# Four mixed blocks on images: operands in DRAM stored once and repeated by the reading transfer

## The chip, the core and the metric

The kernel runs on one core of one Trainium2 chip. The core has five engines that work side by side, each on its own list of instructions in a fixed order: TensorE multiplies matrices, VectorE (DVE) and ScalarE (ACT) work element by element, GpSimd (POOL) does the same and issues transfers, and the sync engine (SP) only issues transfers. They wait for one another through semaphores. Transfers between DRAM and the on-chip memory run on 16 DMA engines, whoever issues them. The metric is the device time of one execution in microseconds. All data are float32.

## The reference

The input is 16 images of 56 x 56 tokens with 128 channels. Four blocks follow, each on a group norm of the image and each added to it: attention in 7 x 7 windows, a triangle multiplication, a Fourier attention over tokens, and a bilinear block with depthwise convolutions. The change touches the end of the third and all of the fourth, which is, cut to what matters:

```
xp = silu(x @ W1) @ W2                 # q: 8 heads x 16, k: 16, v: 16
q, k, v = each normed over its 16 channels
K_H1   = conv3x7(k, H1, depthwise) + P1        # per token 16 x 16
kernel = einsum('xnk,xkd->xnd', q, K_H1)       # 8 x 16
F      = conv3x7(v, H2)                        # per token 16 x 16
V_G    = conv3x7(v, G) + I                     # per token 16 x 16
F      = einsum('xvw,xvd->xwd', V_G, F)
out    = einsum('xnd,xvd->xvn', kernel, F)     # 16 x 8 = 128 channels
```

In the third block the heads' results are sums over products of the image's spectrum with tables of weights, one table for each of 32 heads, the same for all images.

## The kernel before, in words

Images go through all four blocks one by one, and two lanes (even and odd images) have their own buffers, so that instructions of two images are mixed on every engine. The order on each engine is fixed when the program is built: a planner walks through the code with estimated times and places each instruction where it sees it ready. So two images can be in different blocks at the same time. Channels lie on the 128 partitions, tokens along them.

**Tables (third block).** At the start the weights of 32 heads are combined and written to a DRAM tensor `table` (L780, L809), ordered head, chunk, part, position. In the product loop each image runs over 8 chunks `q` and 8 groups `two`; for each, two transfers on GpSimd's queue (L1168) fill 56 partitions each with one copy of two heads' rows, 5376 bytes to a partition, taken from two places in DRAM. VectorE multiplies them with the spectrum (L1173) and TensorE sums.

**Contractions (fourth block).** A chunk is 448 tokens (8 rows), 7 chunks an image. The three einsums of the block all have one form: an operand `y` of 128 rows (a row for each pair of indices) and an operand `z` from a convolution. The products need each row of `y` on 8 partitions. [...] `kept` (L1284) copies `y` out of PSUM and writes it to a DRAM buffer, 8 copies of each row (L1288, on the ACT queue; 1792 KB). `contract` (L1372) then reads it back in four pieces `rep` of 128 partitions x 896 elements (L1381, on the SP queue; 448 KB each, three buffers in turn), VectorE multiplies each with `z` (L1384), and TensorE sums with a 0/1 matrix through the helper at L365 and L368. The sum is the next contraction's `y`. Per chunk there are three such contractions: queries with the key convolution, that result with the value convolution `l3wf`, and that with `l3wg` in `last`.

**Keys and values.** `project(q)` computes queries (kept as above), norms, and the 32 rows of keys and values of a chunk, and writes these to a DRAM tensor `padded` of zero-bordered planes, one plane for each of 32 channels x 3 row shifts x 7 column shifts, 672 in all: three transfers (L1338, on the ACT queue), each writing 7 shifted copies, 434 KB. `spread(q)` (L1344) reads the taps of one chunk back, 84 partitions x 4 groups, for keys and for values (L1347, on the SP queue, 651 KB each) into `im[0]` and `im[1]`, and `conv` (L1352) multiplies them on TensorE (L1362 for `l3wf`, otherwise through L365 and L368) and copies `z` out on ACT (L1369).

**The loop** (end of the block, L1423 on) does in step q: the last contraction of chunk q-2; the projection of chunk q+2; convolution and contraction of `l3wf` and then convolution `l3wg` for chunk q-1; `spread(q)`; convolution `l3wk` and the first contraction for chunk q. At the program's start 672 planes for each of two lanes are filled with zeros (L1256 to L1262).

Of the kernel before, what the change touches and what calls it, by code (L numbers as in the profile page):

```python
# [42 lines left out]
P = 128  # L44
T = 56
# [259 lines left out]
def tile_blocks(ctx: ExitStack, tc: tile.TileContext, ins, out, at, stages=(0, 1, 2, 3)):  # L305
# [41 lines left out]
    def dram():  # L347
        return dyp[lane[0]].tile([P, 8 * CH], F32, tag="dy", name=uid("dy"))
# [365 lines left out]
def _fourier(env):  # L714
# [65 lines left out]
    table = e.dpool.tile([32, 8, 3, STEP], F32, tag="table", name="table")  # L780
# [28 lines left out]
    for c, v in enumerate((cvr, cvi, tmp)):  # L809
        nc.sync.dma_start(out=table[:, :, c, :], in_=v.rearrange("p (c n) -> p c n", n=STEP))  # L810
    sc = W("sc")
    tflat = table.rearrange("h c k n -> h c (k n)")
# [299 lines left out]
    def run(b, xt):  # L1112
# [46 lines left out]
        for q in range(8):  # L1159
# [4 lines left out]
            for two in range(8):  # L1164
                t = slots[n % 8]
                n += 1
                for hh in range(2):
                    nc.gpsimd.dma_start(  # L1168
                        out=t[hh * T : (hh + 1) * T, :].rearrange("p (u n) -> p u n", u=2),
                        in_=bc(tflat[4 * two + hh : 4 * two + hh + 3 : 2, q, :], 0, T),  # L1170
                    )
                t4 = t.rearrange("p (u k n) -> p u k n", u=2, k=3)
                tt(t4, bc(x3[:, :, s], 1, 2), t4, ALU.mult)  # L1173
                prods = [t[:, u * 672 : (u + 1) * 672] for u in range(2)]
                group = []
                for p, k, m in ((pa, 0, 2 * STEP), (pb, 2 * STEP, STEP)):
                    for half in (1, 0):
                        pair = 2 * two + half
                        group.append(
                            dict(  # L1180
                                out=p[64 * half : 64 * half + 64, :m],
                                lhsT=at[:, pair % 8, pair // 8, :],
                                rhs=prods[half][:, k : k + m],
                                start=two == 0,
                                stop=two == 7,
                            )
                        )
                e.together(group)
# [58 lines left out]
def _bilinear(env):  # L1247
# [8 lines left out]
    padded = [e.dpool.tile([P, 672 * PLANE // P], F32, tag=f"padded{k}", name=f"padded{k}") for k in range(2)]  # L1256
    zeros = e.arena()
    part = 672 * PLANE // P // 3
# [9 lines left out]
    def run(b, xt):  # L1268
# [15 lines left out]
        def kept(p):  # L1284
# [3 lines left out]
            nc.scalar.dma_start(out=d.rearrange("p (k t) -> p k t", k=8), in_=bc(t[:, :CH], 1, 8))  # L1288
            return d

        def project(q):
# [45 lines left out]
            for dr in range(3):  # L1337
                nc.scalar.dma_start(  # L1338
                    out=planes(kv_dram, (1 + 8 * q) * PITCH + dr * (7 * PLANE - PITCH), ((21 * PLANE, 32), (PLANE - 1, 7), (1, SPAN))),
                    in_=bc(t, 1, 7),  # L1340
# [3 lines left out]
        def spread(q):  # L1344

            for i in range(2):
                nc.sync.dma_start(  # L1347
                    out=im[i][:84].rearrange("p (g t) -> p g t", g=4),
                    in_=planes(kv_dram, 336 * i * PLANE + q * SPAN, ((PLANE, 84), (84 * PLANE, 4), (1, SPAN))),
# [22 lines left out]
        def contract(y, z):  # L1372

            acc = e.psb()
            yv = y.rearrange("(i n a) (k t) -> n (a k) i t", n=2, a=D, k=8)
            for n in range(2):
                done = []
                for two in (0, 2):
                    rep = reps[count[1] % 3].rearrange("p (i t) -> p i t", i=2)
                    count[1] += 1  # L1380
                    nc.sync.dma_start(out=rep, in_=yv[n][:, two : two + 2, :])  # L1381
# [41 lines left out]
        queries, kern, feat = {q: project(q) for q in range(2)}, {}, {}  # L1423
        for q in range(NCH + 2):
# [4 lines left out]
            if 0 <= q - 1 < NCH:  # L1429
                f = kept(contract(kern.pop(q - 1), conv("l3wf", 1)))  # L1430
                feat[q - 1] = f, conv("l3wg", 1)
            if q < NCH:
                spread(q)
                kern[q] = kept(contract(queries.pop(q), conv("l3wk", 0)))
# [26 lines left out]
```

## Time and profile before

| | |
|---|---|
| time, median of 3 | 15542.86 us (15519.85 to 15596.55) |
| span of the profiled execution | 15563.9 us |
| mean granted TensorE clock | 0.760 |
| DMA bytes | 2251.47 MB, mean 145 GB/s |
| kept operands L1288 | 336 transfers of 1792 KB |
| operand reads L1381 | 1344 of 448 KB |
| keys and values L1338 | 336 of 434 KB |
| taps L1347 | 224 of 651 KB |
| table reads L1168 | 2048 of 294 KB |
| products L1384 on VectorE | 1344 of 2018 ns, 2668.4 us |

A busy share is an average over stages with different limits, so it says little alone. The view of stretches gives the busy time of each engine, the clock and the share of time in which the 16 DMA engines have a packet, for any stretch of the span. The view of waits says for how long an engine stood idle ahead of the instructions of a line, and whose work ended last before it went on; a transfer is written `to<-from`, so `arena<-dy` is a read of a kept operand, `dy<-w` the write, `arena<-padded` a read of taps, and `padded<-arena` the write of keys and values. The chain goes back from the last instruction, at each step to what released it. Packet counts of a queue hold one packet for each contiguous piece and 16 signals for each transfer; q10 is the ACT queue, q1 the SP queue, q0 GpSimd's.

### The profile page before, as it was taken

What the parts mean: (1) busy time and instruction counts of PE and PEld (TensorE: products, weight loads), DVE (VectorE), ACT (ScalarE), POOL (GpSimd) and SP (SyncE); (2) the same over time, 40 slices, a digit from 0 to 9 for tenths busy, and PEclk for the clock granted to TensorE, in tenths of its full rate; (3) what the DMA queues carried; (4) which work ended last, traced back from release to release, by engine and by line L of the source; (5) the groups of instructions that cost most, each with busy time, mean ns of one, the idle gap of its engine ahead of it and who ended that gap; (6) DMA issues with size and microseconds to landing.
All of it is one profiled execution on the core that took longest, in us unless ns stands there. A gap on an engine that the chain in (4) does not pass through costs nothing. (4 is left out here: it accounts for less than half of the span.)

```text
span 15563.9 us, 217025 instructions
## 1 busy us (share of the span) xinstructions
PE 11864.3 (76%) x91360; PEld 6531.3 (42%) x91360; DVE 9494.0 (61%) x13537; ACT 3743.0 (24%) x6251; POOL 1616.6 (10%) x2554
## 2 busy tenths in 40 slices
PE   7887677876888777877778777787777877778675
PEld 4453254443444334534345334453443534435332
DVE  6655666656666656566565665756657566574654
ACT  3222131221321222212222122231221312213111
POOL 0120002200022000210001100111102011020110
PEclk8876787767777678777787777877777777787766
DMA  2356904468145661466533655427465274651747
GB/s 73 79 125 188 299 24 107 110 207 262 34 102 159 189 214 50 98 167 190 170 104 84 190 167 170 135 71 211 129 190 144 57 207 117 190 150 51 217 126 228
DMA packets 1148653, 2251.47 MB, mean 145 GB/s; under 512 B 90656, under 2 KB 1030944, under 8 KB 1145760
## 3 DMA queue, kind: packets, MB, share of 16 engines
q1 hardware_dynamic: 552336, 840.48, 18.4%
q0 software_dynamic: 165120, 629.67, 17.0%
q10 hardware_dynamic: 430224, 767.43, 15.2%
q8 instruction: 722, 11.83, 0.3%
q14 instruction: 251, 2.06, 0.0%
HBM read 1412.72 MB, written 811.60 MB: 143 GB/s over the span
## 5 line engine op out<-in xcount | busy, mean ns | idle before, releaser
L1384 DVE TENSOR_TENSOR arena<-arena 128x1792 f32<-128x1792 f32 x1344 | 2668.4, 2018 | 1468.3 <-DMA arena<-dy 788.1
L368 PE MATMUL psb<-arena,cst 128*32 128x448 f32 (+1 forms) x10368 | 1971.0, 681 | 10.6 <-DVE arena L1216 10.3
L1173 DVE TENSOR_TENSOR arena<-arena 112x1344 f32<-112x1344 f32 x1024 | 1571.1, 1553 | 514.5 <-DMA arena<-table 502.1
L1168 POOL DMA_DIRECT2D arena<-table x2048 | 1326.1, 649 | 3611.6 <-PE psb L1087 990.2
L365 PE MATMUL psb<-arena,cst 128*32 128x448 f32 (+1 forms) x1728 | 1089.8, 720 | 728.1 <-DVE arena L1384 567.9
L368 PE MATMUL psd<-arena 112*64 112x224 f32 (+1 forms) x6144 | 1504.6, 477 | 0.0
L365 PE MATMUL psd<-arena 112*64 112x448 f32 x2048 | 1140.7, 644 | 211.9 <-DVE arena L1173 203.0
L368 PEld LDWEIGHTS psd<-arena 112*64 112x64 f32 x6144 | 617.5, 156 | 605.0 <-issue 596.1
L365 PE MATMUL psd<-arena,wgt 85*32 85x448 f32 x896 | 491.1, 680 | 488.1 <-DMA arena<-padded 486.3
L368 PEld LDWEIGHTS psb<-arena,cst 128*32 128x32 f32 (+1 forms) x10368 | 571.9, 141 | 652.5 <-issue 584.7
L1369 ACT COPY arena<-psd 128x896 f32<-128x896 f32 x336 | 304.2, 905 | 1913.3 <-PE psd L368 930.0
L663 PE MATMUL psd<-wgt,arena 128*64 128x128 f32 x7168 | 616.4, 326 | 164.8 <-DVE arena L675 121.7
L365 PEld LDWEIGHTS psb<-arena,cst 128*32 128x32 f32 (+1 forms) x1728 | 206.6, 154 | 1148.2 <-DVE arena L1384 625.5
L663 PEld LDWEIGHTS psd<-wgt,arena 128*64 128x64 f32 x7168 | 521.0, 165 | 351.7 <-issue 251.1
L1064 DVE TENSOR_TENSOR arena<-w,coef 128x1792 f32<-128x1792 f32 x256 | 507.4, 2019 | 215.6 <-PE psb L368 198.8
L884 PE MATMUL psb<-cst,arena 128*64 128x32 f32 (+1 forms) x10752 | 525.7, 273 | 57.5 <-ACT arena L850 33.7
L1362 PE MATMUL psd<-arena,wgt 85*128 85x448 f32 x896 | 530.8, 753 | 44.2 <-DMA arena<-padded 25.2
L884 PEld LDWEIGHTS psb<-cst,arena 128*64 128x64 f32 x10752 | 511.0, 200 | 125.9 <-issue 54.4
L586 PE MATMUL psb<-cst,arena 128*49 128x128 f32 x2048 | 381.5, 346 | 236.7 <-DVE arena L581 121.9
L368 PE MATMUL psd<-arena,wgt 85*32 85x448 f32 x2688 | 500.4, 681 | 0.0
L368 PE MATMUL psb<-arena 128*64 128x448 f32 x1792 | 498.8, 636 | 0.0
L365 PEld LDWEIGHTS psd<-arena 112*64 112x64 f32 x2048 | 280.1, 156 | 437.8 <-DVE arena L1173 306.6
(290 smaller groups left out, 19342.7 us busy)
## 6 DMA issues: line engine op xcount, KB each, us to landing
arena<-table POOLq DMA_DIRECT2D x2048, 294.0 KB, 9.8
dy<-w ACTq DMA_DIRECT2D x336, 1792.0 KB
arena<-dy SPq DMA_DIRECT2D x1344, 448.0 KB
padded<-arena ACTq DMA_DIRECT2D x336, 434.0 KB
arena<-padded SPq DMA_DIRECT2D x224, 651.0 KB
w<-x SPq DMA_DIRECT2D x112, 224.0 KB
out<-w SPq DMA_DIRECT2D x112, 224.0 KB
padded<-arena SPq DMA_DIRECT2D x6, 3146.5 KB
```

Of the source, the lines that this page charges most:

```text
L365: done = mm(**first)
L368: mm(**kw)
L586: nc.tensor.transpose(p[:WIN, i * P : (i + 1) * P], s3[:, 4 * g + i, :], C("ident"))
L663: mm(p[half : half + 64, i // 4, i % 4 * P : (i % 4 + 1) * P], lhsT=xh[:, c0 : c0 + 64], rhs=W(w).rearrange("p (k c) -> p k c", c=64)[:, : ...
L884: mm(p[64 * c : 64 * c + 64, i * nl : (i + 1) * nl], lhsT=src[:, t * T : t * T + 64], rhs=fc[:, c], start=True, stop=True)
L1064: tt(t4, bc(ys[c][:, l0 : l0 + 4, :], 1, 8), bc(coef[:, c, h0 : h0 + 8, l0 : l0 + 4], 3, T), ALU.mult,)
L1168: nc.gpsimd.dma_start(out=t[hh * T : (hh + 1) * T, :].rearrange("p (u n) -> p u n", u=2), in_=bc(tflat[4 * two + hh : 4 * two + hh + 3 : 2 ...
L1173: tt(t4, bc(x3[:, :, s], 1, 2), t4, ALU.mult)
L1362: mm(p[:, h, :CH], lhsT=wt[:, g * P : (g + 1) * P], rhs=rows[:, g], start=g == 2 * h, stop=g == 2 * h + 1)
L1369: nc.scalar.copy(z, p[:, :, :CH])
L1384: tt(t4, bc(rep, 2, 2), bc(z, 1, 2), ALU.mult)
```

## The change

It keeps in DRAM one copy of each row where there were several, and lets the reading transfer repeat or shift it. A kept operand is written once, ordered by the half n, the row a and the four groups i, so that a piece for one n and two groups i is one contiguous run for each row a, read 8 times. Keys and values are written 3 times (one for each row shift) and not 21 times; the column shift is made by the read, which steps by one element, and each group of taps has its own transfer of 12 planes x 7 shifts. The padded planes are 96, not 672. `spread` takes the tensor (0 keys, 1 values) and is called at other places: the keys of chunk q+1 after the key convolution of chunk q, the values ahead of the contraction with `l3wf`; both value convolutions now come ahead of that contraction. The table is stored so that what a partition takes is one contiguous piece.

```diff
     def dram():
-        return dyp[lane[0]].tile([P, 8 * CH], F32, tag="dy", name=uid("dy"))
+        return dyp[lane[0]].tile([P, CH], F32, tag="dy", name=uid("dy"))
...
-    table = e.dpool.tile([32, 8, 3, STEP], F32, tag="table", name="table")
+    table = e.dpool.tile([8, 8, 2, 2, 3, STEP], F32, tag="table", name="table")
...
     for c, v in enumerate((cvr, cvi, tmp)):
-        nc.sync.dma_start(out=table[:, :, c, :], in_=v.rearrange("p (c n) -> p c n", n=STEP))
+        for k in range(4):
+            nc.sync.dma_start(
+                out=table[:, :, k % 2, k // 2, c, :].rearrange("q w n -> w q n"),
+                in_=v[k:32:4].rearrange("p (q n) -> p q n", n=STEP),
+            )
     sc = W("sc")
-    tflat = table.rearrange("h c k n -> h c (k n)")
+    tflat = table.rearrange("q w h u k n -> q w h (u k n)")
...
                 for hh in range(2):
-                    nc.gpsimd.dma_start(
-                        out=t[hh * T : (hh + 1) * T, :].rearrange("p (u n) -> p u n", u=2),
-                        in_=bc(tflat[4 * two + hh : 4 * two + hh + 3 : 2, q, :], 0, T),
-                    )
+                    nc.gpsimd.dma_start(out=t[hh * T : (hh + 1) * T, :], in_=bc(tflat[q, two, hh], 0, T))
...
-    padded = [e.dpool.tile([P, 672 * PLANE // P], F32, tag=f"padded{k}", name=f"padded{k}") for k in range(2)]
+    padded = [e.dpool.tile([P, 96 * PLANE // P], F32, tag=f"padded{k}", name=f"padded{k}") for k in range(2)]
...
-            nc.scalar.dma_start(out=d.rearrange("p (k t) -> p k t", k=8), in_=bc(t[:, :CH], 1, 8))
+            nc.scalar.dma_start(out=planes(d, 0, ((CH, 4), (4 * CH, 32), (1, CH))), in_=t[:, :CH])
...
                 nc.scalar.dma_start(
-                    out=planes(kv_dram, (1 + 8 * q) * PITCH + dr * (7 * PLANE - PITCH), ((21 * PLANE, 32), (PLANE - 1, 7), (1, SPAN))),
-                    in_=bc(t, 1, 7),
+                    out=planes(kv_dram, (1 + 8 * q) * PITCH + dr * (PLANE - PITCH), ((3 * PLANE, 32), (1, SPAN))),
+                    in_=t,
                 )
...
-        def spread(q):
-
-            for i in range(2):
+        def spread(i, q):
+
+            for g in range(4):
                 nc.sync.dma_start(
-                    out=im[i][:84].rearrange("p (g t) -> p g t", g=4),
-                    in_=planes(kv_dram, 336 * i * PLANE + q * SPAN, ((PLANE, 84), (84 * PLANE, 4), (1, SPAN))),
+                    out=im[i][:84, g * SPAN : (g + 1) * SPAN],
+                    in_=planes(kv_dram, (48 * i + 12 * g) * PLANE + q * SPAN, ((PLANE, 12), (1, 7), (1, SPAN))),
                 )
...
-                    rep = reps[count[1] % 3].rearrange("p (i t) -> p i t", i=2)
+                    rep = reps[count[1] % 3]
                     count[1] += 1
-                    nc.sync.dma_start(out=rep, in_=yv[n][:, two : two + 2, :])
+                    nc.sync.dma_start(out=rep, in_=planes(y, (n * D * 4 + two) * CH, ((4 * CH, D), (0, 8), (1, 2 * CH))))
+                    rep = rep.rearrange("p (i t) -> p i t", i=2)
...
+        spread(0, 0)
         for q in range(NCH + 2):
             if 0 <= q - 2:
                 last(q - 2, *feat.pop(q - 2))
             if q + 2 < NCH:
                 queries[q + 2] = project(q + 2)
             if 0 <= q - 1 < NCH:
-                f = kept(contract(kern.pop(q - 1), conv("l3wf", 1)))
-                feat[q - 1] = f, conv("l3wg", 1)
+                zf, zg = conv("l3wf", 1), conv("l3wg", 1)
             if q < NCH:
-                spread(q)
-                kern[q] = kept(contract(queries.pop(q), conv("l3wk", 0)))
+                spread(1, q)
+            if 0 <= q - 1 < NCH:
+                feat[q - 1] = kept(contract(kern.pop(q - 1), zf)), zg
+            if q < NCH:
+                zk = conv("l3wk", 0)
+                if q + 1 < NCH:
+                    spread(0, q + 1)
+                kern[q] = kept(contract(queries.pop(q), zk))
         return True
```

## The prediction

> **What bounds the kernel now.** I read in this order: busy shares, the stretches by stage, the DMA queues, the waits by line, and the chain that ended last. First the page's busy shares, its queues and its chain by line:
>
> ```profile
> PE 11864.3 (76%) x91360; PEld 6531.3 (42%) x91360; DVE 9494.0 (61%) x13537; ACT 3743.0 (24%) x6251; POOL 1616.6 (10%) x2554
> ...
> q1 hardware_dynamic: 552336, 840.48, 18.4%
> q0 software_dynamic: 165120, 629.67, 17.0%
> q10 hardware_dynamic: 430224, 767.43, 15.2%
> ...
> DMA arena<-table 1%; DMA arena<-dy 1%; DVE arena L1384 1%; DMA arena<-padded 1%; PE psb L368 1%; DMA padded<-arena 0%; PE psb L365 0%; DMA dy<-w 0%; PE psb L884 0%; PE psd L1362 0%; PE psb L1211 0%; PE psd L365 0%; PE psd L663 0%; PE psd L918 0%; PE psb L897 0%
> ```
>
> No engine is full: TensorE is idle 3700 us of 15564. The chain could be followed back over the last ninth of the span only, but there five of its first eight entries are transfers that this change edits. So the average must be split by stage. Six stretches, columns: length, busy PE, PEld, DVE, ACT, POOL, granted clock, DMA share, GB/s:
>
> ```profile
> 2000.00:2400.00 400.00, 326.79 (x3234) 214.09 (x3234) 227.79 (x464) 149.97 (x254) 14.20 (x34) 0.82 0.02 4
> 800.00:1000.00 200.00, 160.49 (x940) 77.67 (x937) 126.00 (x106) 23.50 (x47) 91.66 (x143) 0.81 0.98 217
> 1400.00:1800.00 400.00, 311.50 (x1652) 134.12 (x1644) 252.71 (x273) 65.73 (x112) 0.00 (x0) 0.74 0.93 313
> ...
> 11400.00:11800.00 400.00, 299.23 (x2209) 145.55 (x2209) 247.04 (x294) 95.75 (x138) 4.40 (x10) 0.78 0.70 212
> 15200.00:15560.00 360.00, 205.48 (x1148) 78.11 (x1147) 186.22 (x157) 40.73 (x65) 0.00 (x0) 0.71 0.76 236
> ```
>
> Without transfers (2000 to 2400) TensorE is 82% busy. Where both lanes are in the last block (1400 to 1800) it is 78% with the DMA engines at 93%; with one lane alone at the end it is 57%. Taking all eight stretches that hold the contraction L1384 (1200:2000, 3000:4000, 4900:6000, 6600:8000, 8600:10000, 10400:11800, 12400:13800, 14200:15560), TensorE is busy 7239 of 9860 us, 0.734. The other 5704 us hold the remaining 4625 us, 0.811. The gap between 0.734 and 0.811 is what a change in the last block can be worth. The waits say who makes the gap (us, times, longest):
>
> ```profile
> DVE arena L1384 <- DMA arena<-dy: 788.1, 238, 20.7
> ...
> PE psb L365 <- DVE arena L1384: 567.9, 199, 20.1
> ...
> DVE arena L1173 <- DMA arena<-table: 502.1, 465, 4.2
> PE psd L365 <- DMA arena<-padded: 486.3, 72, 20.1
> ```
>
> VectorE waits for the contraction's operands, TensorE for VectorE's products, and TensorE for the taps of the convolution.
>
> **What the Trainium skill says.** "DMA: Bandwidth & Descriptors", section "Issuing engines are not separate DMA queues": all issuers share the same 16 engines. The trace agrees: in 1400 to 1800 the two hardware queues together fill them to 0.93, so a byte less written is room for a byte read. The same page, section "Why a DMA increments its semaphore by 16 and not by 1": a transfer runs on as many engines, up to 16, as divide the outermost dimensions of both sides. The new kept write has an outermost 4 in DRAM, so by that rule 4 engines; the new tap reads have 12. No run here shows such a transfer. "SBUF — State Buffer", section "Door 1: The DMA port swizzle": half of the partitions reach half of the 16 ports, whose total the page puts at 435 GB/s. A table read fills 56 partitions; the trace has 217 GB/s at a DMA share of 0.98 in 800 to 1000, where nearly all is table reads, just half of that figure.
>
> **The change part by part.**
>
> *Kept operands (L1288).* 21 per image, 1792 KB before, 224 KB after. From the page, q10 spends 15.2% x 16 x 15564 us / 430224 = 88 ns a packet. A kept write is 1024 data packets, 5.6 us of all 16 engines; after it is 128, 0.7 us over 16 engines or 2.8 us if only 4 serve it. I take 2.8 us. In the chain of the last 384 us the write's stretches run from 6.5 to 11.1 us, and the shortest operand reads there are 3.4 us for some 1.5 us of transfer, so 2 us go to the landing; at 2.8 plus 2 each write shrinks by about 4 us. This is serial: products, sums, copy, write, then the reads of the next contraction.
>
> *Keys and values (L1338).* 63 transfers per image, in groups of three; each 434 KB becomes 62 KB, 224 data packets become 32, 1.2 us become 0.2. Queue 10 falls from 430080 to 336 x (144 + 48) = 64512 packets (16 of each transfer are its signals): 365568 x 88 ns / 16 = 2011 us of all 16 engines disappear. Bytes fall by 336 x (1568 + 372) KB = 667 MB of 2251.
>
> *Reads of the contraction (L1381).* 1344 x 448 KB stay; 256 pieces of 1792 bytes become 128 of 3584, read eight times from one row by the repeat. Same bytes, so no gain alone. They gain from emptier engines: at 313 GB/s one takes 1.5 us, and the products take 2.02 us each, so three buffers can keep up when the writes are gone.
>
> *Taps (L1347).* Two transfers of 651 KB become eight quarters. The same 336 pieces of 1984 bytes, now shifted by one element on the read side. Issue rises from 2 to 8 per chunk; at 0.34 us each that is 2 us of a queue that mostly waits, hidden behind its waits for buffers. The old shifted writes were in the 88 ns mean, so I set a shifted read at 88 to 150 ns: 7 per engine on 12 engines, about 1 us per quarter, 4 us for four. Same as before; nothing gained or lost alone.
>
> *Order.* The taps of the key convolution are asked for a chunk ahead and those of the value convolutions before the feature contraction. In the tail the chain has padded writes of 6.2 to 7.6 us, then reads of 5.2 to 10.4 us, then TensorE: some 14 us per chunk that now have other work beside them. A new wait: on the sync queue the tap read for values, waiting for the projection's write, may stand ahead of the four operand reads of the feature contraction, and VectorE waits for those. The old order had the same read ahead of the kernel contraction's four, so the wait moves rather than grows; I cost it at nothing net and keep it as a rival.
>
> *Tables (L1168).* 56 pieces of 5376 bytes from one place instead of two. The trace's packet records already show 5376 bytes per partition, 56 per transfer, so the same bytes go through the same half of the ports: 0. GpSimd's 649 ns an issue may shorten, but its 128 issues per image are 83 us beside 64 products of 1.553 us, 99 us, and beside the transfers.
>
> *Start.* Zeroing falls from 18.9 to 2.7 MB, about 38 us at the 427 GB/s seen there, beside the first block's work: at most 10 us.
>
> *Sum.* The waits above that the edits address are 788 (DVE on operands) and 486 plus 25 (TensorE on taps, L365 and L1362). I take back 80% of the taps' (410), and 60% of the operands' (470) of which 60% reaches the end, since TensorE sometimes has work of the other lane (280). That is 690. The same from densities: contraction stretches at 0.79 instead of 0.734 last 7239 / 0.79 = 9163 us, 697 less. With the start: about 700, so **14840 us**. The lone tail alone gives about 90: 165 us of transfers in its last 384 (the chain's shares of operands 14.5, kept 10.7, taps 10.4, padded 7.4%), of which I leave 75.
>
> **The rivals.**
>
> A: transfers were mostly hidden; VectorE's 2.02 us products, the ACT copy of z (579.9 us of waits at L1384) and the lower clock of a busier TensorE (0.71 to 0.77 in these stretches against 0.82) take the place. For it: in 1200 to 2000, at a share of 0.77, VectorE waits only 100.8 us for operands. A quarter of 1299 us comes back: 325, **15220 us**. Chance 0.20.
>
> B: the gap closes wholly, 7239 / 0.811 = 8926, 934 us less, and a quarter of the 971 us that VectorE and GpSimd wait for tables goes too because the other lane's transfers no longer mix in: **14370 us**. For it: stretches with tables and contractions together reach 0.92 to 0.95. Chance 0.12.
>
> C: slower. The few engines of the kept write and the tap reads become a queue of their own, and the sync queue's wait for the projection (1845.0 us in 123 waits, 15 each) blocks operand reads at 112 chunks; if 5 us more at each and 3 us at each of 336 kept writes end on the path, and only the quarter of rival A is gained, that is 560 + 1008 - 325 = +1243 at worst; with a fifth of it, **15790 us**. Against it: even on 4 engines a kept write takes half of what it took. Chance 0.08.
>
> **Numbers.** The forecast has 0.60, with a spread of 14550 to 15150. The range reaches from a little below B to beyond A: 14300 to 15400, leaving out C and the ends, under 0.2. Faster by over 0.5% (below 15465): the forecast, B and most of A, 0.89; same 0.04; slower 0.07.
>
> **What would show it.** Right: bytes near 1570 MB and q10 near 65000 packets; DVE's wait for operands at 300 us or less, TensorE's wait for taps at 100 or less; TensorE near 0.79 in the contraction stretches; the last lone stretch shorter by about 90 us; table reads still at about 217 GB/s where they stand alone. Wrong: if operands still hold VectorE over 600 us at a DMA share below 0.5 (a wait for latency or issue order, not bandwidth), if the wait at L1384 turns to the copy of z, or if the clock falls as TensorE fills.

## The result

| | before | after |
|---|---|---|
| time, median | 15556.48 us (15519.85 to 15596.55, 4 runs) | 15133.76 us (15076.72 to 15160.78, 4 runs) |
| span of the profiled execution | 15563.9 us | 15153.5 us |
| mean granted TensorE clock | 0.760 | 0.777 |
| DMA bytes | 2251.47 MB | 1567.45 MB |

The ratio is 0.9723, with a 95% interval of 0.9683 to 0.9763: the change takes 2.8% off, 423 us between the medians. The forecast was 700 us. The direction and the range hold, two fifths of the gain are missing (277 of 700 us), and the profile shows in which wait.

The page of the kernel after: busy shares, packets and the ACT queue's line.

```profile
PE 11727.6 (77%) x91360; PEld 6416.4 (42%) x91360; DVE 9489.1 (63%) x13537; ACT 3749.5 (25%) x6257; POOL 1322.8 (9%) x2554
...
DMA packets 614696, 1567.45 MB, mean 103 GB/s; under 512 B 94288, under 2 KB 324944, under 8 KB 612560
...
q10 hardware_dynamic: 60624, 99.93, 2.5%
```

Bytes went as worked out, and packets nearly so. TensorE's idle time fell from 3700 to 15153.5 - 11727.6 = 3426 us, by 274. The other 137 us of the 410 by which the spans differ is busy time: the same 91360 matmuls took 11727.6 instead of 11864.3 us, at a higher clock. (Busy time does not follow the clock alone: four_writes, below, has 11790.2 us at 0.779.)

One number on q10 holds more than it seems. The prediction expected 64512 packets, 16 signals for each of 672 transfers; the page has 60624, some 3900 fewer. If each of the 336 kept writes has 4 signals and not 16, that is 336 x 12 = 4032 fewer, 60480; the other 144 are on the page of before too (430224, where 430080 were worked out). So the count of packets alone says that the new write has 4 signals, and if each engine signals once, it runs on 4 engines. Nor has every other transfer 16: the sync queue's 4-byte packets (28752 before, 36416 after) fit 16 for each operand read, 14 for each old tap read and 12 for each new one. The rest is then 4112 and 4160, and tables_only shows that the 48 more are the new table writes' (28800).

The waits of the kernel after, by line (us, times, longest):

```profile
PE psb L364 <- DVE arena L1384: 1131.0, 312, 21.5
...
DVE arena L1384 <- DMA arena<-dy: 1125.6, 366, 23.1
...
DVE arena L1173 <- DMA arena<-table: 505.8, 484, 10.5
...
DVE w L1294 <- DMA dy<-w: 161.7, 29, 23.2
...
DVE arena L1384 <- ACT arena L1369: 73.6, 16, 17.5
...
PE psd L364 <- DMA arena<-padded: 41.8, 18, 7.1
...
PE psd L367 <- DMA arena<-padded: 36.6, 17, 4.5
```

The wait for the copy of z in the kernel before:

```profile
DVE arena L1384 <- ACT arena L1369: 579.9, 61, 23.9
```

TensorE's wait for taps fell from 511 to 78 us, as forecast. VectorE's wait for the copy of z fell from 579.9 to 73.6, which was not forecast. z is computed from the taps, and over the runs below the two waits go together (805.5 for z and 698.6 for taps in kept_only, 688.1 and 542.0 in tables_only, 83.8 and 47.2 in old_order). But VectorE's wait for operands **rose**, from 788.1 to 1125.6 us. It was to fall to 300. In sum VectorE stands idle ahead of its products as long as before: 1468.3 us in the group of L1384 before, 1443.4 after. The wait changed hands, from the copy of z to the operand's transfer (all_but_kept, below, shows this without the operands' new form), and TensorE's wait for the products doubled (567.9 to 1131.0). A kept write now also holds VectorE elsewhere, at L1294 (161.7, before 2.8), where a work buffer comes free only when the write that reads it has landed.

The stretches of the kernel after that hold L1384 (length, busy PE, PEld, DVE, ACT, POOL, granted clock, DMA share, GB/s):

```profile
1200.00:2000.00 800.00, 575.30 (x4089) 272.13 (x4089) 533.70 (x708) 179.25 (x320) 21.81 (x38) 0.78 0.51 139
3000.00:4000.00 1000.00, 741.61 (x5798) 379.70 (x5795) 631.28 (x912) 253.95 (x424) 37.56 (x44) 0.76 0.41 112
...
14000.00:15153.00 1153.00, 764.20 (x4920) 360.02 (x4918) 656.08 (x754) 178.04 (x298) 71.19 (x137) 0.73 0.49 129
sum 9153.00, PE 6817.94 PEld 3453.57 DVE 5687.92 ACT 2112.39 POOL 509.81; mean PE 852.24 PEld 431.70 DVE 710.99 ACT 264.05 POOL 63.73
```

The DMA engines are half empty there now, and TensorE's density is 6817.94 / 9153 = 0.745; the forecast was 0.79, from 0.734. Operands hold VectorE over 600 us at a DMA share near 0.5 or below, which is nearly word for word a sign that the prediction gave of being wrong, a wait for latency or issue order and not for bandwidth. But this share is an average of the stretch. Summed over the packets that fall into VectorE's waits for operands alone, the 16 engines are busy 0.73 of the time: 0.48 with the operand reads themselves, 0.13 with taps, 0.08 with tables, 0.04 with writes (before it was 0.88 in all, 0.28 of it writes). So the engines have room on the average, and VectorE still waits in bursts that its own reads fill for a good part; the share alone does not tell the latency of a read from the length of its transfer.

From the chain in order of time, last 374 us of the kernel after, where one lane is left (start, us, what; the longest pieces):

```profile
15042.42 5.08 DMA arena<-dy
15047.62 2.02 DVE arena L1384
15051.67 2.03 DVE arena L1384
15053.72 6.66 DMA arena<-dy
15060.51 2.04 DVE arena L1384
15062.56 5.74 DMA arena<-dy
15068.43 2.03 DVE arena L1384
15070.48 5.43 DMA arena<-dy
```

A read comes right after a product ends, since with three buffers it can only start when the product three back has released its own. It then has two more products to hide behind, 2 x 2.02 = 4.04 us, and it takes 5.1 to 6.7. So it shows, again and again. In this stretch the chain's share of operand reads is 25.6%, 96 us, against 14.5% of 384 us, 56 us, before; kept writes fell from 41 to 24 us and taps from 40 to 16.

What these transfers cost to issue (minimum, median, maximum in ns), first before, then after:

```profile
L1381 SPq DMA_DIRECT2D arena<-dy x1344: 359/360/2839, 1243.3 to 15549.2; - x192
```

```profile
L1347 SPq DMA_DIRECT2D arena<-padded x224: 308/337/2038, 1298.6 to 15460.9; - x112
```

```profile
L1380 SPq DMA_DIRECT2D arena<-dy x1344: 514/515/2051, 1154.5 to 15136.6; - x192
```

```profile
L1347 SPq DMA_DIRECT2D arena<-padded x896: 751/756/1991, 1189.8 to 15052.9; - x180
```

A repeated read costs the sync engine 155 ns more than the old one, a shifted tap read more than twice the old. From the start of the issue to the end of the last packet, by the trace's packet records (medians), an operand read went from 3.86 to 4.40 us although the engines are emptier; its 128 pieces of 3584 bytes took 202 ns each, where two of 1792 had taken 2 x 74. The times of single packets are skewed, and by their means the two forms lie closer, 210 against 2 x 94. A kept write went from 8.6 to 6.0 us, with one eighth of the bytes.

### The profile page after: what moved, and what is told of

The parts are those of the page before. It is cut to its first block, busy times and chain, and to the rows that moved or that the text cites. A ratio compares the mean times of both kernels' runs of the same rounds, so it can differ in the third digit from the quotient of the medians.

```text
span 15153.5 us, 218547 instructions
## 1 busy us (share of the span) xinstructions
PE 11727.6 (77%) x91360; PEld 6416.4 (42%) x91360; DVE 9489.1 (63%) x13537; ACT 3749.5 (25%) x6257; POOL 1322.8 (9%) x2554
## 2 busy tenths in 40 slices
DMA packets 614696, 1567.45 MB, mean 103 GB/s; under 512 B 94288, under 2 KB 324944, under 8 KB 612560
## 3 DMA queue, kind: packets, MB, share of 16 engines
q10 hardware_dynamic: 60624, 99.93, 2.5%
## 5 line engine op out<-in xcount | busy, mean ns | idle before, releaser
L1384 DVE TENSOR_TENSOR arena<-arena 128x1792 f32<-128x1792 f32 x1344 | 2676.7, 2019 | 1443.4 <-DMA arena<-dy 1125.6
L364 PE MATMUL psb<-arena,cst 128*32 128x448 f32 (+1 forms) x1728 | 1127.3, 743 | 1288.1 <-DVE arena L1384 1131.0
L367 PE MATMUL psb<-arena,cst 128*32 128x448 f32 (+1 forms) x10368 | 2067.2, 722 | 7.7 <-DVE arena L1216 6.5
L1173 DVE TENSOR_TENSOR arena<-arena 112x1344 f32<-112x1344 f32 x1024 | 1573.0, 1553 | 529.9 <-DMA arena<-table 505.8
L367 PE MATMUL psd<-arena 112*64 112x224 f32 (+1 forms) x6144 | 1465.2, 469 | 0.0
L1171 POOL DMA_DIRECT2D arena<-table x2048 | 1057.5, 519 | 3789.4 <-PE psd L367 1057.9
L367 PEld LDWEIGHTS psd<-arena 112*64 112x64 f32 x6144 | 614.9, 154 | 587.6 <-issue 576.6
L662 PE MATMUL psd<-wgt,arena 128*64 128x128 f32 x7168 | 542.8, 299 | 92.2 <-DVE arena L674 75.9
L662 PEld LDWEIGHTS psd<-wgt,arena 128*64 128x64 f32 x7168 | 465.6, 149 | 230.8 <-issue 168.2
L1287 ACT COPY w<-psb 128x448 f32<-128x448 f32 x336 | 178.7, 532 | 1535.9 <-PE psb L367 1214.8
L1362 PE MATMUL psd<-arena,wgt 85*128 85x448 f32 x896 | 440.6, 643 | 11.7 <-ACT arena L1369 9.9
```

The source lines that it names most:

```text
L364: done = mm(**first)
L367: mm(**kw)
L662: mm(p[half : half + 64, i // 4, i % 4 * P : (i % 4 + 1) * P], lhsT=xh[:, c0 : c0 + 64], rhs=W(w).rearrange("p (k c) -> p k c", c=64)[:, : ...
L1171: nc.gpsimd.dma_start(out=t[hh * T : (hh + 1) * T, :], in_=bc(tflat[q, two, hh], 0, T))
L1287: nc.scalar.copy(t[:, :CH], p[:, :CH])
L1362: mm(p[:, h, :CH], lhsT=wt[:, g * P : (g + 1) * P], rhs=rows[:, g], start=g == 2 * h, stop=g == 2 * h + 1)
```

## The experiments

Three theories. **Theory 1**: the latency of the operand's path keeps the gain small: the write runs on four engines, and the repeated read is slower to issue and to move. **Theory 2**: the sync queue blocks, since tap reads (dearer to issue, waiting for the projection) stand ahead of operand reads. **Theory 3**: the planner makes other lists for each version, and that alone moves the time. Ratios are against runs of the kernel before on the same chip, with 95% intervals; "points" are hundredths of that ratio. The change itself stands at 0.9723.

### Parts alone, lists planned anew

**kept_only**: the kernel before with the kept operands' new write and read, nothing else.

```diff
...
-    nc.scalar.dma_start(out=d.rearrange("p (k t) -> p k t", k=8), in_=bc(t[:, :CH], 1, 8))
+    nc.scalar.dma_start(out=planes(d, 0, ((CH, 4), (4 * CH, 32), (1, CH))), in_=t[:, :CH])
...
-    nc.sync.dma_start(out=rep, in_=yv[n][:, two : two + 2, :])
+    nc.sync.dma_start(out=rep, in_=planes(y, (n * D * 4 + two) * CH, ((4 * CH, D), (0, 8), (1, 2 * CH))))
```

> The kernel before with the kept operands alone changed (written once, read eight times from one row); keys, values, taps, order of the loop and tables as before. Theory 1 (latency of the operands: the write runs on few engines and still takes about 6 us, the reads land later than before): little, 15300 to 15500 us, with VectorE's wait for operands not below 700 us and TensorE's wait for taps still near 500. Theory 2 (the sync queue: eight tap reads of 0.76 us issue and the wait for the projection stand ahead of operand reads): without the new taps the gain of the kept operands shows in full, 15000 to 15200 us, operands' wait below 500 us. Bandwidth alone, as predicted: about 15200.

Measured: 15982.61 us, ratio 1.029 (1.0266 to 1.0314). Slower, and outside the range of every theory. The waits of this kernel:

```profile
DVE arena L1384 <- DMA arena<-dy: 890.4, 281, 17.4
...
DVE arena L1384 <- ACT arena L1369: 805.5, 68, 26.5
...
PE psd L365 <- DMA arena<-padded: 698.6, 78, 20.0
```

The waits for the copy of z and for taps rose by 226 and 212 us, though the edit touches neither. So this run does not price the edit; it was the first sign of Theory 3.

**all_but_kept**: the kernel after with the kept operands' write and read as they were before (the two lines above, reversed).

> The changed kernel with the kept operands as before (eight copies written, distinct rows read). Theory 1: the taps and their order bring the larger part, 15150 to 15300 us; TensorE's wait for taps below 120 us, VectorE's wait for operands 700 to 900. Theory 2: the new order of the sync queue hurts whatever the operands' form, 15400 to 15600 us, and VectorE's wait for operands over 1000 us.

Measured: 14998.36 us, ratio 0.9664 (0.9645 to 0.9684), 0.6 points better than the whole change and below the range of either theory. VectorE's waits:

```profile
DVE arena L1384 <- DMA arena<-dy: 1018.9, 286, 22.3
...
DVE arena L1384 <- ACT arena L1369: 88.1, 10, 18.9
```

The part that was to save the most bytes brings no time between these two sets of lists, each planned anew. And VectorE waits 1018.9 us for operands although their form is the old one. So 231 of the 338 us by which this wait rose come with the rest of the change and its lists: with the taps in time z is in time, and VectorE then waits for what had been hidden behind z, the operand.

**old_order**: the kernel after with the loop of before.

```diff
-        spread(0, 0)
...
-                zf, zg = conv("l3wf", 1), conv("l3wg", 1)
+                f = kept(contract(kern.pop(q - 1), conv("l3wf", 1)))
+                feat[q - 1] = f, conv("l3wg", 1)
             if q < NCH:
+                spread(0, q)
                 spread(1, q)
-            if 0 <= q - 1 < NCH:
-                feat[q - 1] = kept(contract(kern.pop(q - 1), zf)), zg
-            if q < NCH:
-                zk = conv("l3wk", 0)
-                if q + 1 < NCH:
-                    spread(0, q + 1)
-                kern[q] = kept(contract(queries.pop(q), zk))
+                kern[q] = kept(contract(queries.pop(q), conv("l3wk", 0)))
```

> The changed kernel with the loop in its old order (both tap reads of a chunk together, after the projection; value convolutions where they stood). Theory 1: the order frees TensorE, so without it TensorE's wait for taps comes back to 300 to 500 us and the time rises to 15300 to 15450 us. Theory 2: the new order is what blocks operand reads, so without it the time falls, to 14900 to 15100 us.

Measured: 15287.69 us, ratio 0.9848 (0.9828 to 0.9868). TensorE's waits for taps are 47.2, 25.6 and 17.3 us, about as small as with the new order: the layout with 96 planes takes that wait away by itself, which Theory 1 had not expected. Nor did the time fall, as Theory 2 had it, and VectorE's wait for operands is 1287.0 us, more than with the new order. The new order goes with 1.25 points, of which the planner's lists may be a part.

**four_writes**: the kernel after with the kept write as four transfers of 32 partitions each.

```diff
-            nc.scalar.dma_start(out=planes(d, 0, ((CH, 4), (4 * CH, 32), (1, CH))), in_=t[:, :CH])
+            for i in range(4):
+                nc.scalar.dma_start(out=planes(d, i * CH, ((4 * CH, 32), (1, CH))), in_=t[32 * i : 32 * i + 32, :CH])
```

> The changed kernel with each kept operand written by four transfers of 32 partitions, each with an outermost dimension of 32, not by one with an outermost 4; same bytes, same layout, same reads. Theory 1: the one write runs on 4 engines (its packets overlap 3.2 to 3.8 times in the trace), 4.2 us from first to last packet; four writes use 16 and land in about 3 us from the issue of the first, 3 us sooner at 336 places: 14850 to 15050 us. Theory 2: nothing changes on the sync queue: 15100 to 15200 us, or slower by the 1.5 us more that ACT's queue spends on issues (336 x 1.5 = 500 us of ACT's list).

Measured: 14899.18 us, ratio 0.9596 (0.9575 to 0.9616), 1.3 points better than the change, with the same bytes. Each of the four now takes 2.2 us from its issue to its last packet, and all four together 4.5 us from the first issue, against 6.0 for the one write (3 were expected). The operand wait fell to 930.6 us and TensorE's wait for products to 887.7. For Theory 1, with the planner's freedom beside it.

**tables_only**: the kernel before with the new table and its reads alone.

```diff
-    table = e.dpool.tile([32, 8, 3, STEP], F32, tag="table", name="table")
+    table = e.dpool.tile([8, 8, 2, 2, 3, STEP], F32, tag="table", name="table")
...
-                    nc.gpsimd.dma_start(
-                        out=t[hh * T : (hh + 1) * T, :].rearrange("p (u n) -> p u n", u=2),
-                        in_=bc(tflat[4 * two + hh : 4 * two + hh + 3 : 2, q, :], 0, T),
-                    )
+                    nc.gpsimd.dma_start(out=t[hh * T : (hh + 1) * T, :], in_=bc(tflat[q, two, hh], 0, T))
```

> The kernel before with the table's order alone changed. On the chip it should cost and bring nothing but 0.13 us less issue on GpSimd, which mostly waits: 15520 to 15580 us by all theories of the hardware. Theory 3: the planner lays out all lists anew (nearly every line of them moves), so a difference of up to 1.5% to either side can come from that alone, 15300 to 15750 us; its size tells how far other comparisons without a held order can be trusted.

Measured: 15448.61 us, ratio 0.9941 (0.9921 to 0.9961). A table packet of 5376 bytes took 304 ns at the median, 355 before; VectorE's wait for tables fell from 502.1 to 389.4 us. How much of the 0.6 points is tables and how much other lists is not separated.

### The same edits with the lists held

In these four each engine's list was built first with the DMA form of one kernel, and then, in a second build, every instruction was tied to its place in that list while the transfers in question took another form; the cuts show the first form and the second. The traces bear it out: VectorE's 13537 instructions come in the same order, by operation and tiles, in the change, fix_contig, fix_overlap and fix_both, and again in the kernel before and fix_kept, while kept_only has another instruction than the kernel before at 8969 places. No run held the lists and left the form alone, so what the holding itself does was not measured by itself.

**fix_kept**: the lists of the kernel before, with the edit of kept_only.

> The kernel before with the kept operands changed as in kept_only, but every engine's list held to the order of the kernel before, so that the planner decides nothing. Theory 3 (kept_only lost its 2.9% to another order of the lists, which the planner made from other estimates): 15250 to 15500 us, no slower than before, since the write lands 2.6 us sooner and the DMA engines have half the bytes. Theory 1 (the compact form itself costs: repeated reads are slower, four engines carry the writes): 15750 to 16000 us with the old order too.

Measured: 15374.58 us, ratio 0.9911 (0.9879 to 0.9944). The waits of this kernel:

```profile
DVE arena L1394 <- DMA arena<-dy: 547.2, 239, 17.8
...
DVE arena L1394 <- ACT arena L1373: 516.8, 56, 24.3
...
PE psd L366 <- DMA arena<-padded: 419.8, 63, 20.9
```

The same edit costs 2.9 points when the planner may rearrange and gains 0.9 when it may not. **Theory 3 is shown**: 3.8 points, some 590 us, lie between two lists of the same work. On the old lists the single copy does what it was meant for: the operand wait falls by 241 us and the time by about 140. VectorE's wait for a kept write at L1294's instruction (here L1298) rises meanwhile from 2.8 to 184.7 us.

**fix_contig**: the lists of the kernel after; the kept write goes to 128 rows in one run. The rows then lie in another order, so the contraction takes other rows than the reference's.

```diff
-    nc.scalar.dma_start(out=planes(d, 0, ((CH, 4), (4 * CH, 32), (1, CH))), in_=t[:, :CH])
+    nc.scalar.dma_start(out=d, in_=t[:, :CH])
```

> The changed kernel with its own order of all lists held, and the kept write made as one contiguous run of 128 rows, so an outermost dimension of 128 instead of 4; same bytes, same reads (the rows then stand in another order than the reads assume, so the output isn't the reference's). Theory 1: the write lands in about 2.5 us from its issue instead of 6, 3.5 us sooner at 336 places, a third to a half of them on the path: 14700 to 14950 us. Theory 3 (order is what matters): 15050 to 15150 us, as the changed kernel.

Measured: 14649.96 us, ratio 0.943 (0.939 to 0.947): **2.9 points better than the change**, with the same bytes and lists, and 50 us below Theory 1's range. The page of this kernel, first its busy shares, then its queue of kept writes:

```profile
PE 11533.2 (79%) x91360; PEld 6349.7 (43%) x91360; DVE 9495.5 (65%) x13537; ACT 3751.2 (26%) x6257; POOL 1324.2 (9%) x2554
...
q10 hardware_dynamic: 64656, 99.95, 2.1%
```

Its wait for operands:

```profile
DVE arena L1388 <- DMA arena<-dy: 756.9, 337, 20.5
```

The queue has 64656 - 60624 = 4032 packets more, 336 x 12: now each write has 16 signals. Issue to last packet fell from 6.0 to 2.87 us, the transfer alone from 4.2 to 1.6. In the change's write the packets overlap 3.4 times at the median and in nine of ten writes under 3.8 times, as four engines would make them. The operand wait fell from 1125.6 to 756.9 us and that at L1294's instruction from 161.7 to 76.1.

**fix_overlap**: the lists of the kernel after; each operand read takes 128 distinct runs, 444 elements apart, instead of 16 runs eight times each. It contracts other data.

```diff
-    nc.sync.dma_start(out=rep, in_=planes(y, (n * D * 4 + two) * CH, ((4 * CH, D), (0, 8), (1, 2 * CH))))
+    nc.sync.dma_start(out=rep, in_=planes(y, 0, ((444, P), (1, 2 * CH))))
```

> The changed kernel with its own order of all lists held, and each operand read taking 128 runs of 896 elements at 128 different places 444 elements apart, with an outermost dimension of 128 on both sides, not 16 rows eight times each; same bytes, same size of pieces (other data, so the output isn't the reference's). Theory 1: if the repeat is what slows the 3584-byte pieces (median 202 ns, at best 140), they fall to 140 to 160 ns, a read lands 0.5 us sooner and the issue falls from 0.515 to about 0.36 us: 14950 to 15080 us. If the size of the piece or the load is the cause: pieces still near 200 ns and 15100 to 15160 us.

Measured: 14889.8 us, ratio 0.9592 (0.9548 to 0.9636), 1.3 points better than the change and 60 us below Theory 1's range. The issue of the reads in this kernel, and VectorE's wait for them:

```profile
L1384 SPq DMA_DIRECT2D arena<-dy x1344: 319/320/1723, 1150.2 to 14911.0; - x192
```

```profile
DVE arena L1388 <- DMA arena<-dy: 928.5, 304, 18.2
```

So the repeat costs 195 ns of issue. A piece of 3584 bytes took 140 ns at the median instead of 202 (180 instead of 210 on the mean), and a read 3.78 us instead of 4.40. The two, issue and slower pieces, were not told apart.

**fix_both**: the two edits together.

> The changed kernel's lists held, with both of the forms tried singly before: the kept write goes to 128 rows in one run (rows in another order), and the operand reads take 128 distinct runs 444 elements apart instead of 16 runs eight times each. What it contracts is therefore not the reference's data. Theory 1 (latency of the operand path is what keeps the gain small): singly they gave 484 and 244 us below the changed kernel's 15134. If the two latencies add on the same serial path, 14400 to 14480, and VectorE's wait for operands falls to about 550 to 650 us from 1125.6. Theory 4 (they hide behind one another, since what ends an operand's wait is then another thing: the products' buffers, the copy of z, the granted clock): no better than the write alone, 14600 to 14700. The kernel before, 15525, would then have been beaten by 7% with the same bytes as the change.

Measured: 14390.04 us, ratio 0.9281 (0.9239 to 0.9324), 4.4 points better than the change; singly they gave 2.9 and 1.3. They add up, so Theory 4 (the two latencies hide behind one another) falls. An effect of holding the lists would stand twice in the sum of the single gains and once in this one; 4.2 and 4.4 leave no room for more than a few tenths of a point. The waits of this kernel:

```profile
DVE arena L1391 <- DMA arena<-dy: 569.3, 243, 20.8
```

**Theory 1 is shown in this sense**: with the lists held and the bytes the same, the form of two transfers is worth 4.4 points, about 690 us. That is more than the 294 us by which the forecast was missed. It says what a better form of the single copy gives, not that the form chosen is worse than eight copies: on the old lists it gained 0.9 points (fix_kept).

**Theory 2** got no run of its own. Against its first form, the issue, stands a count in the trace of the kernel after: of the 1125.6 us in which VectorE waits for operands, 1034 pass after the read has been issued, 17 while it is issued, and 75 before, only 20 of these while the sync engine issues taps. But a read that is issued right behind taps also has their packets beside it. In the kernel after, the 298 reads issued within 4 us of a tap read took 5.2 us from issue to last packet (medians), the others 4.1, and 618 of the 1125.6 us are waits for these 298; in the kernel before there were 51 such reads, with 54 of 788 us. In fix_both 448 of the 569 us left are of this kind. Such reads are often the first of a contraction, too, so how much of this is the taps is not shown. In this second form Theory 2 stays open.

### More buffers

**four_five**: four_writes with five buffers for the reads instead of three, and three for the products instead of four. The whole computation.

```diff
-        reps = [ar[:, 6656 + k * 896 : 7552 + k * 896] for k in range(3)]
-        prods = [ar[:, 9344 + k * 1792 : 11136 + k * 1792] for k in range(4)]
+        reps = [ar[:, 6656 + k * 896 : 7552 + k * 896] for k in range(5)]
+        prods = [ar[:, 11136 + k * 1792 : 12928 + k * 1792] for k in range(3)]
...
```

> The changed kernel with the kept write as four transfers of 32 partitions (as in four_writes, 14899) and five buffers for the operand reads instead of three, three for the products instead of four; the whole computation. Theory 1: more reads in flight hide the 4.4 us of a read behind products of 2.02 us each; three buffers let two reads run ahead, 4.04 us, so they nearly keep up already while the order allows; what more buffers add is the first read of a contraction only where the operand is written early. 14650 to 14850, VectorE's operand wait 600 to 850 us from 930.6. Theory 3 (lists): with other buffers the planner makes other lists, and that alone can move the time by some per cent, so 14500 to 15400 with no fall of the operand wait that would account for it.

Measured: **14426.34 us, ratio 0.9305** (0.9282 to 0.9327), below the ranges of both theories: 4.2 points better than the change, and the best version here that computes the whole. VectorE's waits:

```profile
DVE arena L1173 <- DMA arena<-table: 551.6, 495, 15.7
DVE arena L1385 <- DMA arena<-dy: 525.4, 248, 15.2
DVE arena L1385 <- PE psb L367: 408.2, 211, 10.4
```

The operand wait has halved against the change. The third line is the price of three product buffers: VectorE now waits for TensorE to release one.

**five_reps**: the same edit to the kernel after, without the four writes.

> The changed kernel with five buffers for the operand reads instead of three and three for the products instead of four, all else as in the change; the whole computation. It is the same edit as between four_writes and four_five, on other lists. Theory 1: 14850 to 15050 from 15134, operand wait 800 to 1000 us from 1125.6, and the same sign and about the same size as between the other two. Theory 3: the two differences disagree in sign or by more than 200 us, since the lists are planned anew each time.

Measured: 14981.83 us, ratio 0.9655 (0.9633 to 0.9676), 0.7 points better than the change; operand wait 837.4 us. So the buffers took 405 us of operand wait in one pair and 288 in the other, as Theory 1 has it, but 2.9 points of time in one and 0.7 in the other. The sign is the same; the difference of 2.2 points, some 345 us, is over the 200 that were set for Theory 3. How much of four_five's gain is buffers and how much a lucky list stays open. The buffers were not tried on held lists.

## Why the prediction was right and where it failed

**Bytes, packets, keys and values: right.** 1567.45 MB for about 1570. The write of keys and values fell from 5.1 to 1.37 us, issue to last packet.

**Taps: right in the gain, wrong in two prices.** The wait fell by 433 us (forecast 410), and the layout does it, not the order. A quarter's issue was set at 0.34 us and takes 0.756, so 896 of them hold the sync engine 677 us and not 305; the count above finds only 20 us of that ahead of VectorE. A quarter's transfer was set at about 1 us and took some 1.4 from first to last packet (median); what that costs the operand reads behind it is open.

**Order: not shown to be nothing net.** Rival C's wait for the projection ahead of the reads did not come in size: 75 us pass before a read is issued. But the reads that stand right behind taps carry over half of the operand wait, and old_order shows that the new order was worth up to 1.25 points by another way.

**Kept write: the mis-sized term.** 4.8 us were forecast (2.8 and 2 to land), 6.0 measured from the issue, so it shrank by 2.6 us and not by 4. The prediction had the reason in hand. The Trainium skill, "DMA: Bandwidth & Descriptors", section "Why a DMA increments its semaphore by 16 and not by 1", gives the engines of a transfer as the largest number up to 16 that divides the outermost sizes of both sides; the outermost 4 means 4, and the trace agrees, with 3.4 packets at once and 4 signals. The prediction chose 4 engines and then took 88 ns a packet, 32 x 88 = 2.8 us. Measured were 4.2 us from the first packet to the last, 131 ns for each of 32 in turn, while a packet itself took 107 ns on the mean (74 at the median), so part of it is time between packets. The page's same section says that such a transfer takes the lowest-numbered engines; no run here shows which they were. Whether every kept write then stands behind other transfers on the same four is not shown either. fix_contig prices this choice at 2.9 points.

**Operand reads: the step that failed.** "Same bytes, so no gain alone", 1.5 us each, "three buffers can keep up when the writes are gone". Of the 280 us that this step was to give, none came as shorter operand waits; they rose by 338. Two things were wrong in it. First, the sum took back the wait for taps and the wait for operands as if each stood by itself. But z and the operand are needed by the same product, so with z in time VectorE waits for the operand instead, in the old form too (1018.9 us in all_but_kept). Where z stays late, in fix_kept, the new form does take 241 us off the operand wait, of 470 forecast. Second, bytes were the wrong measure of a read. Reading one row eight times made a piece slower than two separate ones (202 against 148 ns at the median, 210 against 187 on the mean), the issue rose from 0.360 to 0.515 us, and a read took 2.4 us from first packet to last and 4.40 from its issue, on emptier engines. And the bound for three buffers is 4.04 us from issue to landing, not the time of the transfer alone: the prediction's own profile had 3.4 us as the shortest read, already close to it. How the 338 us divide between the two, the taps beside the reads and the new lists is open.

**The z copy and the clock: rival A's reasons fell the other way.** A's 15220 us is the nearest number of all, 86 us off. But its mechanism is not what happened: the copy of z holds VectorE 506 us less, and the clock rose. The prediction read the lower clock of the contraction's stretches as the price of a fuller TensorE, though they are less busy by its own figures (0.734 against 0.811). The Trainium skill, "TensorE: Matmul & The Clock Gate", section "Part 1: The HAM clock gate (the "warmup" mystery)", says the opposite, that activity releases the throttle, and over whole kernels the runs go that way: 0.750 at a busy share of 75% (kept_only), 0.760 at 76% (before), 0.777 at 77% (after), 0.790 at 79% (fix_contig), 0.796 at 80% (fix_both), with four_writes as an exception, 0.779 at 79%. The stretches of before do so only in part: 0.82 at 82% busy without transfers and 0.71 at 57% in the last, but also 0.74 at 78% and 0.78 at 75%. No run varied the clock alone, so that the busy share is the cause is not shown. If the page's reason holds, a wait removed pays twice, and some of the 137 us of busy time here are of that second kind.

**The tail: wrong.** The lone stretch was to shrink by 90 us. As the windows of the chain are cut it went from 384 to 374 us, and from the other lane's last store to the last store of all from 602 to 593, since 40 us more of reads took back what kept writes and taps gave.

**Tables: cost nothing, as said, and gave a little.** A packet went from 355 to 325 ns, GpSimd's issue from 645 to 514 ns. But the reading of 217 GB/s as a ceiling was wrong. In this stretch of the kernel after, nearly all is table reads again (26.02 of 26.08 MB):

```profile
700.00:800.00 100.00, 71.82 (x424) 36.58 (x424) 74.43 (x65) 4.15 (x12) 46.04 (x87) 0.82 0.88 261
```

That is 261 GB/s at a lower DMA share than the 0.98 of before. And the two transfers of a pair fill partitions 0 to 55 and 56 to 111, so the second one does not stay in one half of the partitions, as the prediction's argument needs. VectorE's wait for tables is unchanged, 505.8 for 502.1, and what the faster reads are worth in time is not separated (tables_only).

**What no step held: the lists.** The sum added up waits as if the instructions stayed in their places. kept_only against fix_kept shows 3.8 points between two plans of the same edit, more than the change itself. So 423 us is the sum of at least three things: taps and z given, operand latency taken, and a list that no reading of the kernel before could tell. The size of the last in the change itself is open, so it is in part luck that the total fell inside the range.

## What to carry to other kernels

Before bytes are taken out of a write, ask whether its reader waits for bandwidth or for a landing; if for a landing, count the engines of each transfer by its outermost size and the time from issue to landing against what the buffers can hide (buffers less one, times the consumer's instruction). A single copy that is re-read eight times moves less and can still arrive later; here, writing it as four wide transfers and giving the reads five buffers turned 2.8% into 7%, with the lists planned anew. Two waits that end at the same instruction are not two gains: when one goes, look for the other behind it. Where a planner orders the lists, an edit is priced only with the lists held, else some per cent that belong to the lists go with it.

## What the runs showed of the hardware

- One DRAM row read eight times by one transfer: 202 ns for a piece of 3584 bytes, 140 ns for pieces of the same size that all start at different places (fix_overlap, fix_both). These are medians; the means are 210 and 180.
- The issue of a transfer on the sync and ACT queues differs with its shape at the same bytes (medians): for reads of 448 KB 320 ns with 128 equal steps, 360 in the old form and 515 with a repeat in it; for writes of 224 KB 344 in one run and 517 with an outermost 4. A tap read of 163 KB with 12 planes x 7 shifts took 756.
- A kept write with one eighth of the bytes on a quarter of the engines saved only 2.0 of 6.2 us of transfer; the same bytes on 16 engines took 1.6.
- Table reads nearly alone moved 217 GB/s at a DMA share of 0.98 when each partition's 5376 bytes came from two places, and 261 at 0.88 when they came from one (stretches 800 to 1000 before, 700 to 800 after).
- Over versions with the same matmuls TensorE's mean granted clock rose with its busy share, from 0.750 at 75% to 0.796 at 80%, with one exception (four_writes, 0.779 at 79%).
